# Linear attention and a 4-bit MLP on one core: the q and k projections as three one-pass products of exact 12-bit pieces

## The chip, the core and the metric

The kernel runs on one core of a Trainium2 chip. A core has a tensor engine (TensorE, PE in the profile, with its weight loads as PEld), a vector engine (DVE), a scalar engine (ACT), GpSimd (POOL) and a sync engine (SP), which here only issues DMA transfers. Each engine runs its own instructions in order and waits for the others through semaphores. SBUF is the working memory of 128 partitions; PSUM has eight banks and takes the results of TensorE. The metric is the device time of one execution in microseconds.

## The reference

Input x is (4, 512, 512): four batches of 512 tokens with 512 features. Two residual blocks follow each other, each on a layer norm of its input.

```python
# block 1: gated linear attention, 4 heads of 128, chunks of 128 tokens
q = (x @ Wq + bq); k = (x @ Wk + bk); v = (x @ Wv + bv)          # each 512 x 512
k = k / max(norm(k, axis=-1), 1e-12)                              # per head
alpha = sigmoid(x @ Walpha + balpha); beta = softplus(x @ Wbeta + bbeta)
# per chunk: attn = (q k^T) * beta * decay, causal;  y = attn v + (q state) * chunk_decay
#            state = state * total_decay + v^T (k * beta * decay_to_end)
# block 2: 4-bit GEGLU MLP, 512 -> 4096 -> 512
inter = gelu(x @ Wg.T) * (x @ Wu.T);  out = inter @ Wd.T
```

Wg, Wu and Wd come as 4-bit numbers with a scale per 32 elements, and are unpacked on the chip.

## The kernel before

The program has one list of steps, counted by `p`. The first 48 belong to the attention projections, 12 for each of the four batches `b`: steps `j` 0 to 3 compute v for one token tile of 128 (`product_v`), 4 to 7 compute q transposed for one head (`product_q`), 8 to 11 compute k for one token tile (`product_k`). Behind each step `behind(p)` emits the work of the attention chunk, which lags nine steps and takes three steps: with `p % 3 == 0` the transposed k (`chunk_lead`) and the decays (`chunk_decay`), with 1 the scores (`chunk_scores`), with 2 the sums (`chunk_sums`), the next chunk's factors (`chunk_values`) and the norm of the finished tile (`second_norm`). From batch 1 on the normed rows are turned by two DMA passes through DRAM and a DVE transpose (`cross`, `turn_blocks`); batch 0 and the second norm use TensorE transposes (`turn`). So the program's order on each engine is written by hand, and nothing else plans it.

The projections are float32 matmuls. The transposed normed rows of a batch stand in `hT[b]`, two tiles of 128 x 2 x 512; v (L425, L432) has them as stationary operand with 128 tokens, q (L450) has Wq as the stationary and all 512 tokens as the moving operand, k (L474) has the tokens stationary and Wk moving. ACT evicts q with its bias (L454), DVE evicts v (L440, L441) and k (L480).

The MLP follows. It works in rounds over the batches, with each gate/up tile (`gate_up`) as products that are already one-pass: the weights and the activations are split in three float32r pieces `hi`, `lo` and `mi`, and

```python
            for o, js in ((pa, (0, 1)), (pb, (2,))):
                for j in js:
                    for k in range(KC):
```

(L849 to L851) makes 8 + 4 matmuls in two PSUM banks; ACT takes `pb` with a factor (L858), DVE adds `pa` (L859). The first gate/up steps lie inside batch 3: after `j == 9` of that batch two steps of the MLP are put in, and from step 50 on only the MLP is left.

The MLP's weights are unpacked in the meantime. `fetch` loads one set of packed numbers and scales, `more` takes three `two_k` tiles for it if there are three (L243), and `unpack` emits one of the set's steps a call: `fields` (L162, two instructions), `masked` (L167), `scaled` (L171), `hi` on ACT (L177) with `lo` (L180), and `mi` (L183). Until step 49 `unpack` is called at L1080, in two steps of three from step 13 on.

SBUF tiles come from two lists of slots, `two_k` (24 of 128 x 2 x 512) and `one_k` (42 of 128 x 512, which borrow from `two_k` when they run out). A slot is handed out in the order in which it came free, and its new writer waits for the old readers. The eight PSUM banks go round in order too.

The functions that the change touches, and what calls them:

## Time and profile before

| | us |
|---|---|
| median of 3 runs | 1301.86 (1300.24 to 1302.41) |
| span of the profiled execution | 1299.2 |
| around the span, to the median | 2.7 |
| TensorE busy | 1287.6 |
| vector engine busy | 968.7 |
| q matmuls, L450 (64 in the program, 128 recorded) | 57.6 |
| k matmuls, L474 (64, 128 recorded) | 57.4 |
| last k matmul starts at | 234.2 |

For the profiled execution the profile gives the span from its first to its last instruction as its own time; what lies around it is taken as the distance to the median of the runs. The granted clock of TensorE is 1.00 throughout.

How to read the profile: the chain of work that ended last goes back from the last instruction to what released it, and its share by line says which line's time the program's time is made of. A table of stretches gives each engine's busy time between two points of the span. A timeline row has its start, its duration, the engine, the line, and how long the engine had been idle before it and for whom. Every float32 matmul is recorded as two instructions. Matmuls are pipelined, and their ends are modelled: the spacing of the chain's pieces says more than the single durations.

### The profile page before, as it was taken

Reading aid. Unit: us, or ns where it says so; the run is one execution under the profiler, and the core shown is the slowest. Engines: PE = TensorE matmul, PEld = TensorE weight load, DVE = VectorE, ACT = ScalarE, POOL = GpSimd, SP = SyncE. Lnnn points to the kernel's source line nnn. Section 1 sums busy time; section 2 is a strip of 40 time slices with the busy share of each in tenths; the row PEclk is TensorE's granted clock in tenths of the full one; section 3 lists DMA queues with packets and bytes.
Section 4 is the critical chain, followed back from the end, with each engine's and each line's share of the span. In section 5 each row is a group of like instructions: output and inputs, shape, how many; then the busy total and the mean of one; then the engine's idle time right before and its main releaser. Section 6 shows DMA issues by size and latency. Waiting matters only on the chain.

```text
span 1299.2 us, 17045 instructions
## 1 busy us (share of the span) xinstructions
PE 1287.6 (99%) x5736; PEld 1030.2 (79%) x5736; DVE 968.7 (75%) x1581; ACT 451.8 (35%) x878; POOL 113.1 (9%) x179
## 2 busy tenths in 40 slices
PE   9999999999999999999999999999999999999998
PEld 6667576778888888888888888888888888887886
DVE  4577865887777777777777777777777777777566
ACT  2433335743333333333333333333333333332332
POOL 1536362400000000000000000000000000000000
PEclk9999999999999999999999999999999999999999
DMA  6556667986565656565656565656565556555473
GB/s 206 148 168 196 191 196 223 314 279 205 179 195 178 195 178 195 178 195 178 195 178 195 178 194 179 195 178 195 178 194 179 192 181 192 180 179 199 167 253 126
DMA packets 195383, 250.24 MB, mean 193 GB/s; under 512 B 16672, under 2 KB 93792, under 8 KB 195296
## 3 DMA queue, kind: packets, MB, share of 16 engines
q1 hardware_dynamic: 195296, 249.16, 59.7%
q8 instruction: 45, 0.74, 0.2%
q14 instruction: 42, 0.34, 0.1%
HBM read 191.91 MB, written 57.18 MB: 192 GB/s over the span
## 4 chain that ended last, share of the span: by engine, by line
PE 95%; DMA 2%; DVE 1%; ACT 1%; SPq 0%; issue 0%; POOL 0%; DVEq 0%; ACTq 0%
PE pa L853 35%; PE p_d L897 26%; PE pb L853 17%; PE pq L450 4%; PE pk L474 4%; PE pvb L432 2%; PE pva L425 2%; PE yp L717 1%; PE sp L663 1%; PE yp L719 1%; PE dp L688 1%; PE tp_f L380 1%; DMA wvb<-in_Wv 0%; DMA x<-h 0%; DMA acc<-acc 0%
## 5 line engine op out<-in xcount | busy, mean ns | idle before, releaser
L853 PE MATMUL pa<-x,wgu 128*128 128x512 f32 x2048 | 507.1, 390 | 0.1
L853 PEld LDWEIGHTS pa<-x,wgu 128*128 128x128 f32 x2048 | 383.9, 188 | 79.5 <-DVE acc L909 0.4
L897 PE MATMUL p_d<-wd,i 128*128 128x512 f32 x1542 | 357.3, 389 | 2.3 <-DVE xr L726 0.6
L897 PEld LDWEIGHTS p_d<-wd,i 128*128 128x128 f32 x1542 | 288.3, 188 | 65.7 <-DVE i L877 2.1
L858 ACT ACTIVATE t<-pb 128x512 f32<-128x512 f32 x256 | 151.3, 591 | 356.5 <-PE pb L853 353.6
L853 PE MATMUL pb<-x,wgu 128*128 128x512 f32 x1024 | 273.8, 389 | 0.0
L859 DVE TENSOR_TENSOR t<-pa,t 128x512 f32<-128x512 f32 x256 | 176.6, 690 | 81.0 <-ACT t L858 75.7
L853 PEld LDWEIGHTS pb<-x,wgu 128*128 128x128 f32 x1024 | 192.3, 188 | 40.0
L905 DVE SCALAR_TENSOR_TENSOR acc<-p_d,acc 128x512 f32<-128x512 f32 (+1 forms) x137 | 93.4, 683 | 125.5 <-PE p_d L897 123.8
L873 ACT ACTIVATE i<-t 128x512 fp32r<-128x512 f32 x128 | 81.0, 633 | 194.3 <-DVE t L870 191.2
L865 ACT ACTIVATE t<-t 128x512 f32<-128x512 f32 x128 | 81.1, 634 | 136.2 <-DVE t L859 136.2
L877 DVE TENSOR_TENSOR i<-t,i 128x512 fp32r<-128x512 f32 x128 | 88.4, 691 | 25.9 <-ACT i L873 24.1
L909 DVE TENSOR_TENSOR acc<-acc,p_d 128x512 f32<-128x512 f32 x135 | 92.9, 688 | 14.4 <-PE p_d L897 0.5
L870 DVE SCALAR_TENSOR_TENSOR t<-t,t 128x512 f32<-128x512 f32 x128 | 88.6, 692 | 4.3
L928 POOL TENSOR_TENSOR acc<-acc,last 128x512 f32<-128x512 f32 x1 | 1.3, 1295 | 1015.0 <-ACT last L927 1015.0
L878 DVE SCALAR_TENSOR_TENSOR i<-i,t 128x512 fp32r<-128x512 f32 x128 | 89.0, 695 | 0.0
L450 PE MATMUL pq<-hT,wq 128*128 128x512 f32 x128 | 57.6, 595 | 0.0
L474 PE MATMUL pk<-wk,hT 128*128 128x512 f32 x128 | 57.4, 593 | 0.0
L450 PEld LDWEIGHTS pq<-hT,wq 128*128 128x128 f32 x128 | 23.6, 191 | 24.1 <-issue 23.9
L474 PEld LDWEIGHTS pk<-wk,hT 128*128 128x128 f32 x128 | 23.3, 191 | 23.9 <-issue 23.9
L183 DVE TENSOR_TENSOR wgu<-wgu,wgu 128x1024 fp32r<-128x1024 f32 x32 | 38.9, 1216 | 0.0
L180 DVE SCALAR_TENSOR_TENSOR wgu<-wgu,w_gu 128x1024 fp32r<-128x1024 f32 x32 | 38.9, 1215 | 0.0
(120 smaller groups left out, 902.0 us busy)
## 6 DMA issues: line engine op xcount, KB each, us to landing
x<-h SPq DMA_DIRECT2D x420, 256.0 KB
acc<-acc SPq DMA_DIRECT2D x256, 256.0 KB
h<-g SPq DMA_DIRECT2D x48, 256.0 KB
x<-in_x SPq DMA_DIRECT2D x16, 256.0 KB
pk_gu<-in_gate_p SPq DMA_DIRECT2D x32, 128.0 KB
sc_gu<-in_gate_s SPq DMA_DIRECT2D x64, 64.0 KB
pk_gu<-in_up_p SPq DMA_DIRECT2D x32, 128.0 KB
sc_gu<-in_up_s SPq DMA_DIRECT2D x64, 64.0 KB
```

The costliest lines, as they stand in the source:

```text
L450: nc.tensor.matmul(pq, f32(wq[k // 2])[:, k % 2, h * P : (h + 1) * P], f32(hT[b][k // 2])[:, k % 2, :], start=(k == 0), stop=(k == KC - 1),)
L474: nc.tensor.matmul(pk, f32(hT[b][k // 2])[:, k % 2, n * P : (n + 1) * P], f32(wk[k // 2])[:, k % 2, :], start=(k == 0), stop=(k == KC - 1),)
L853: nc.tensor.matmul(o, w3[j][:, k % 2, c * P : (c + 1) * P], x[j * KC + k], start=(j == js[0] and k == 0), stop=(j == js[-1] and k == KC - 1),)
L858: nc.scalar.activation(f32(t), pb, AF.Copy, scale=-1.0 / ONE_E)
L859: nc.vector.tensor_tensor(f32(t), pa, f32(t), ALU.add)
L865: nc.scalar.activation(f32(g), f32(g), AF.Gelu_apprx_tanh, scale=ONE_E)
L870: nc.vector.scalar_tensor_tensor(f32(u), f32(g), ONE_E, f32(u), ALU.mult, ALU.mult)
L877: nc.vector.tensor_tensor(il, f32(u), f32(ih), ALU.subtract)
L878: nc.vector.scalar_tensor_tensor(im, f32(ih), ONE_E, f32(u), ALU.mult, ALU.subtract)
L897: nc.tensor.matmul(banks[key_][:, part], inter[i][j][:, n * P : (n + 1) * P], wd[ms[i] // 2][j][:, ms[i] % 2, part], start=(i == 0 and j i ...
L905: nc.vector.scalar_tensor_tensor(a, banks[n, False, part.start][:, part], ONE_E, a, ALU.mult, ALU.add)
L909: nc.vector.tensor_tensor(a, a, banks[n, True, 0], ALU.subtract)
```

## The change

q and k are computed like the MLP's gate and up products. The operands are split into pieces of 12 bits: `hi` is the operand rounded to 12 bits by ACT's output type, `lo` is the rest, and `mi` is `hi` less the (scaled) rest, so that hi·hi + lo·lo (in `pa`) and mi·mi (in `pb`) together give the product. `three` makes 12 one-pass matmuls for each product where 4 float32 matmuls stood.

- The transposed normed rows of a token tile go to a raw `one_k` tile `rows_of[b, n]`; v takes it as it is. `pieces` makes `hi` (ACT), `lo` and `mi` (both DVE) from it, in halves of 128 x 256, for four token tiles in the steps 0, 1, 2 and 2 of a batch. `hT[b]` becomes six `two_k` tiles instead of two. `read` frees the raw tile when v and the pieces have read it.
- `split` makes the pieces of Wq in steps 1 and 2 of batch 0 (128 x 1024 at a time: ACT, DVE, POOL), and those of Wk in steps 4 to 7 (128 x 512 at a time). Wq's pieces are six `two_k` tiles, Wk's are twelve `one_k` tiles; the raw ones come free.
- q's eviction becomes an ACT instruction on `pb` and a DVE instruction on `pa`. k's becomes an ACT instruction on `pb`, a POOL addition of the bias and a DVE addition of `pa`; k is left with a factor that the norm takes away.
- `two_k` has 25 tiles. `more` starts a set of MLP weights only if `kept` further `two_k` tiles are free, and from step 40 on `unpack` is called twice in two steps of three and once in the third.

```diff
@@ -117,7 +117,7 @@
                 else:
                     self.free.append(tag)
 
-    two_k = Homes("a", 24, [P, 2, T])
+    two_k = Homes("a", 25, [P, 2, T])
     one_k = Homes("b", 42, [P, T], two_k)
 
     def psum(name):
@@ -240,7 +240,7 @@
 
     def more():
 
-        if not loaded or len(two_k.free) < 3:
+        if not loaded or len(two_k.free) < 3 + kept(place[0]):
             return
         nxt, start = loaded.pop(0)
         fields, masked, scaled, hi, lo, mi = start()
@@ -273,6 +273,50 @@
     VA = D + 2 * H - D // 2
     VB = D - VA
     acc, hT, q_sb, k_sb, v_sb = {}, {}, {}, {}, {}
+    rows_of, half_read = {}, set()
+
+    def kept(p):
+
+        if p > 3 * NCH * (B - 1) + NCH:
+            return 2 if p < 3 * NCH * B else 0
+        return H // 2 + (3 * KC // 2 if p % (3 * NCH) == 0 and p < 3 * NCH * B else 0)
+
+    def split(hi, lo, mi, w):
+
+        nc.scalar.activation(hi, w, AF.Copy, scale=HI * E12)
+        nc.vector.scalar_tensor_tensor(lo, f32(hi), -4096.0, w, ALU.mult, ALU.add)
+        nc.gpsimd.tensor_tensor(mi, f32(hi), f32(lo), ALU.subtract)
+
+    def pieces(b, n):
+
+        if n == 0:
+            hT[b] = [[two_k.get(f"h{j}_{b}_{c}") for c in range(KC // 2)] for j in range(3)]
+        r = rows_of[b, n]
+        for c in range(KC // 2):
+            hi, lo, mi = (hT[b][j][c][:, :, n * P : (n + 1) * P] for j in range(3))
+            w = f32(r)[:, 2 * c * P : 2 * (c + 1) * P].rearrange("p (two t) -> p two t", two=2)
+            nc.scalar.activation(hi, w, AF.Copy, scale=HI * 4096.0)
+            nc.vector.scalar_tensor_tensor(lo, w, 4096.0, f32(hi), ALU.mult, ALU.subtract)
+            nc.vector.scalar_tensor_tensor(mi, f32(hi), E12, f32(lo), ALU.mult, ALU.subtract)
+        read(b, n)
+
+    def read(b, n):
+
+        if (b, n) in half_read:
+            one_k.put(rows_of.pop((b, n)))
+        half_read.add((b, n))
+
+    def three(key, w, x, soon=False):
+
+        pa, pb = psum(f"pa_{key}"), psum(f"pb_{key}")
+        for o, js in ((pa, (0, 1)), (pb, (2,))) if soon else ((pb, (2,)), (pa, (0, 1))):
+            for j in js:
+                for k in range(KC):
+                    nc.tensor.matmul(
+                        o, w(j, k), x(j, k),
+                        start=(j == js[0] and k == 0), stop=(j == js[-1] and k == KC - 1),
+                    )
+        return pa, pb
 
     def round_now():
         while rounding:
@@ -382,20 +426,17 @@
             use(tp)
 
     def first_norm(b, n, src, within=None):
-        if n == 0:
-            hT[b] = [two_k.get(f"hT{b}_{c}") for c in range(KC // 2)]
-
         soon = b == n == 0
 
         def use(tp):
-            for c in range(KC // 2):
-                to = f32(hT[b][c])[:, :, n * P : (n + 1) * P]
-                new = tp[:, 2 * c * P : 2 * (c + 1) * P].rearrange("p (two t) -> p two t", two=2)
-                for part in ((0, 1), (1, 2)) if soon else ((0, 2),):
-                    nc.scalar.copy(to[:, slice(*part), :], new[:, slice(*part), :])
+            r = rows_of[b, n] = one_k.get(f"r_{b}_{n}")
+            w = P if soon else D
+            for i in range(0, D, w):
+                nc.scalar.copy(f32(r)[:, i : i + w], tp[:, i : i + w])
 
         def way(t):
-            turn_blocks(t, *(f32(hT[b][c])[:, :, n * P : (n + 1) * P] for c in range(KC // 2)))
+            r = rows_of[b, n] = one_k.get(f"r_{b}_{n}")
+            turn_blocks(t, heads(f32(r)))
 
         norm(src, f"a{b}_{n}", use, 2 if soon else 1, within, way if b > 0 else None)
 
@@ -419,20 +460,21 @@
 
     def product_v(b, n, between=None):
 
-        toks = slice(n * P, (n + 1) * P)
+        r = f32(rows_of[b, n])
         pa, pb = psum(f"pva_{b}_{n}"), psum(f"pvb_{b}_{n}")
         for k in range(KC):
             nc.tensor.matmul(
-                pa[:, :VA], f32(hT[b][k // 2])[:, k % 2, toks], f32(wva[k // 2])[:, k % 2, :VA],
+                pa[:, :VA], r[:, k * P : (k + 1) * P], f32(wva[k // 2])[:, k % 2, :VA],
                 start=(k == 0), stop=(k == KC - 1),
             )
         if between:
             between()
         for k in range(KC):
             nc.tensor.matmul(
-                pb[:, : VB + 2 * H], f32(hT[b][k // 2])[:, k % 2, toks], wvb_[:, k, :],
+                pb[:, : VB + 2 * H], r[:, k * P : (k + 1) * P], wvb_[:, k, :],
                 start=(k == 0), stop=(k == KC - 1),
             )
+        read(b, n)
         v = one_k.get(f"v_{b}_{n}")
         v_sb[b, n] = v
         if n == 0:
@@ -445,15 +487,15 @@
 
         if h == 0:
             q_sb[b] = [two_k.get(f"q{b}_{c}") for c in range(H // 2)]
-        pq = psum(f"pq_{b}_{h}")
-        for k in range(KC):
-            nc.tensor.matmul(
-                pq, f32(wq[k // 2])[:, k % 2, h * P : (h + 1) * P], f32(hT[b][k // 2])[:, k % 2, :],
-                start=(k == 0), stop=(k == KC - 1),
-            )
-        nc.scalar.activation(
-            f32(q_sb[b][h // 2])[:, h % 2, :], pq, AF.Identity, bias=bq_sb[:, h : h + 1]
+        pa, pb = three(
+            f"q_{b}_{h}",
+            lambda j, k: wq[j][k // 2][:, k % 2, h * P : (h + 1) * P],
+            lambda j, k: hT[b][j][k // 2][:, k % 2, :],
+            b == h == 0,
         )
+        q = f32(q_sb[b][h // 2])[:, h % 2, :]
+        nc.scalar.activation(q, pb, AF.Identity, bias=bq_sb[:, h : h + 1], scale=-1.0)
+        nc.vector.scalar_tensor_tensor(q, pa, ONE_E, q, ALU.mult, ALU.add)
 
     def far(b, n):
 
@@ -469,15 +511,18 @@
 
     def product_k(b, n):
 
-        pk = psum(f"pk_{b}_{n}")
-        for k in range(KC):
-            nc.tensor.matmul(
-                pk, f32(hT[b][k // 2])[:, k % 2, n * P : (n + 1) * P], f32(wk[k // 2])[:, k % 2, :],
-                start=(k == 0), stop=(k == KC - 1),
-            )
+        pa, pb = three(
+            f"k_{b}_{n}",
+            lambda j, k: hT[b][j][k // 2][:, k % 2, n * P : (n + 1) * P],
+            lambda j, k: wk[j][k],
+        )
+        t = one_k.get(f"kt_{b}_{n}")
+        nc.scalar.activation(f32(t), pb, AF.Copy, scale=-1.0 / ONE_E)
+        nc.gpsimd.tensor_tensor(f32(t), f32(t), f32(bk_sb), ALU.add)
         kt = one_k.get(f"k_{b}_{n}")
         k_sb[b, n] = kt
-        nc.vector.tensor_tensor(heads_of(kt, far(b, n)), in_blocks(pk), in_blocks(f32(bk_sb)), ALU.add)
+        nc.vector.tensor_tensor(heads_of(kt, far(b, n)), in_blocks(pa), in_blocks(f32(t)), ALU.add)
+        one_k.put(t)
         if far(b, n):
 
             def use(t):
@@ -498,7 +543,7 @@
                 AF.Square, accum_out=sn[:, h : h + 1],
             )
         one_k.put(sq)
-        nc.gpsimd.tensor_scalar(sn, sn, 1e-24, None, ALU.max)
+        nc.gpsimd.tensor_scalar(sn, sn, 1e-24 / ONE_E**2, None, ALU.max)
         nc.gpsimd.tensor_tensor(sn, sn, minus_half, ALU.pow)
         brn = small.tile([P, H], F32, tag="brn", name=f"brn{b}_{n}")
         nc.gpsimd.tensor_tensor(brn, sn, beta[b][:, n * H : (n + 1) * H], ALU.mult)
@@ -1005,6 +1050,7 @@
         wvb = two_k.get("wvb")
         wvb_ = f32(wvb).rearrange("p two (k n) -> p (two k) n", n=VB + 2 * H)
         wq, wk = ([two_k.get(f"w{nm}{c}") for c in range(KC // 2)] for nm in "qk")
+        raw_q, raw_k = wq, wk
         x0 = [load(tile_of(n), f"x0_{n}") for n in range(2)]
 
         busy = psum("busy")
@@ -1043,6 +1089,8 @@
         turn("a", 1)
         blocks = mlp()
         p = 0
+        wq = [[two_k.get(f"wq{j}_{c}") for c in range(KC // 2)] for j in range(3)]
+        wk = [[one_k.get(f"wk{j}_{k}") for k in range(KC)] for j in range(3)]
         for b in range(B):
             for j in range(3 * NCH):
                 later = None
@@ -1061,23 +1109,47 @@
                     product_q(b, j - NCH)
                 else:
                     later = product_k(b, j - 2 * NCH)
+                if b == 0:
+                    if 0 < j < 3:
+                        split(*(wq[i][j - 1] for i in range(3)), f32(raw_q[j - 1]))
+                        two_k.put(raw_q[j - 1])
+                    if j < 3:
+                        pieces(0, j)
+                    if j == 2:
+                        pieces(0, 3)
+                    if j == NCH:
+                        nc.gpsimd.tensor_scalar(f32(bk_sb), f32(bk_sb), 1.0 / ONE_E, None, ALU.mult)
+                    if NCH <= j < 2 * NCH:
+                        k = j - NCH
+                        split(*(wk[i][k] for i in range(3)), f32(raw_k[k // 2])[:, k % 2, :])
+                        if k % 2:
+                            two_k.put(raw_k[k // 2])
+                elif j < 3:
+                    pieces(b, j)
+                    if j == 2:
+                        pieces(b, 3)
                 if b == B - 1:
                     if j == NCH - 1:
                         two_k.put(*wva, wvb)
                         one_k.put(bv_sb)
                     elif j == 2 * NCH - 1:
-                        two_k.put(*wq)
+                        for ws in wq:
+                            two_k.put(*ws)
                     elif j == 3 * NCH - 1:
-                        two_k.put(*wk)
+                        for ws in wk:
+                            one_k.put(*ws)
                         one_k.put(bk_sb)
                 if j == 3 * NCH - 1:
-                    two_k.put(*hT[b])
+                    for hs in hT[b]:
+                        two_k.put(*hs)
                 behind(p)
                 if later:
                     later()
                 if p in (5, 7):
                     fetch()
-                if p > 3 * NCH and p % 3:
+                if p > 3 * NCH * (B - 1) + NCH - 1:
+                    unpack(2 if p % 3 else 1, MT)
+                elif p > 3 * NCH and p % 3:
                     unpack(1, MT)
                 p += 1
                 if b == B - 1 and j in (2 * NCH - 4, 2 * NCH - 3):
```

## The prediction

> **What bounds the kernel now.** I read the page's busy shares first, then the chain, then the stretches of the attention stage, then the tensor engine's timeline beside the vector engine's.
>
> ```profile
> PE 1287.6 (99%) x5736; PEld 1030.2 (79%) x5736; DVE 968.7 (75%) x1581; ACT 451.8 (35%) x878; POOL 113.1 (9%) x179
> ...
> PE 95%; DMA 2%; DVE 1%; ACT 1%; SPq 0%; issue 0%; POOL 0%; DVEq 0%; ACTq 0%
> PE pa L853 35%; PE p_d L897 26%; PE pb L853 17%; PE pq L450 4%; PE pk L474 4%; PE pvb L432 2%; PE pva L425 2%; PE yp L717 1%; PE sp L663 1%; PE yp L719 1%; PE dp L688 1%; PE tp_f L380 1%; DMA wvb<-in_Wv 0%; DMA x<-h 0%; DMA acc<-acc 0%
> ```
>
> TensorE (PE) is busy 99% of 1299.2 us and carries 95% of the chain; the products that change (L450, L474) carry 8% of it. All of them lie before 235 us. The chain prices one product of each kind, the float32 ones and the three one-pass products of the MLP (L853), whose shapes the new ones take:
>
> ```profile
> 45.70 3.44 PE pk L474 x8
> ...
> 50.02 3.44 PE pk L474 x8
> ...
> 276.98 1.81 PE pa L853 x8
> 278.79 0.91 PE pb L853 x4
> ...
> 280.13 1.85 PE pa L853 x8
> 281.98 0.91 PE pb L853 x4
> ```
>
> 3.44 us for four float32 matmuls (recorded as eight), 2.72 to 2.76 us for twelve one-pass matmuls. What pays for it is the vector engine (DVE). The stretches (columns: start and end, length, then busy time with the number of instructions of PE, PEld, DVE, ACT and POOL, the granted clock, DMA) show the first batch from its first q product, the four three-step cycles of the second, and the place where attention ends and the MLP starts:
>
> ```profile
> 23.70:38.40 14.70, 14.70 (x39) 6.56 (x39) 6.81 (x30) 5.78 (x12) 0.55 (x1) 1.00 0.33 92
> 38.40:55.28 16.88, 16.88 (x61) 9.19 (x61) 5.87 (x13) 7.05 (x36) 6.96 (x14) 1.00 0.63 170
> 55.28:70.25 14.97, 14.97 (x89) 13.48 (x88) 10.18 (x27) 4.48 (x16) 10.78 (x17) 1.00 0.47 143
> 70.25:84.60 14.35, 14.35 (x69) 10.02 (x68) 12.16 (x31) 4.58 (x11) 5.92 (x7) 1.00 0.62 184
> 84.60:99.03 14.43, 14.43 (x60) 8.14 (x59) 10.94 (x29) 7.04 (x20) 3.38 (x5) 1.00 0.57 172
> 99.03:112.88 13.85, 13.85 (x57) 8.03 (x56) 10.12 (x20) 6.00 (x32) 10.92 (x19) 1.00 0.81 221
> ...
> 200.50:273.00 72.50, 69.11 (x338) 49.52 (x337) 53.34 (x97) 44.24 (x110) 24.12 (x37) 1.00 0.85 274
> ```
>
> TensorE never stops in the first six; DVE is busy 68% to 85% of the second batch, and the last stretch already holds 3.4 us of stalled TensorE.
>
> **The sum.** It is made against the profiled execution: span 1299.2 us, and 2.7 us more to the median of the runs, 1301.86, which I leave as they are.
>
> *Products.* 16 q and 16 k products go from 3.44 to 2.74 us: 32 x 0.70 = 22.4 us gained, all on the path. The v products keep their instructions. [...]
>
> *Prices on DVE.* By distance of starts in its timeline: 128x256 with two inputs 0.34 us (L440 to L441), 128x512 0.61 (L407 to L408), 128x1024 1.1 (L180 to the next). New there: `pieces`, 4 of 128x256 per token tile, 16 x 0.34 = 5.4 us a batch; the second half of q's eviction, 4 x 0.61 = 2.4 a batch; once, `lo` of Wq, 2 x 1.1, and of Wk, 4 x 0.61. One 128x512 transpose in place of two halves returns 0.07 a tile. ACT's part (0.6 for a 128x512 copy, some 6 us a batch) lies beside its 35%.
>
> *The added wait.* k's addition on DVE (L480) now waits for ACT's copy (0.6, L858) and POOL's bias (1.04 to 1.30, L642 and L928) of the part that TensorE ends 1.85 us before the other. They fit, if POOL is free. Behind the addition stand on DVE the chunk's sum (L726) and the norm's statistics; ACT's squares (L496) and the transposes of k (L593) wait for it, the latter a whole product (2.7 us) later. That cover makes it nothing; without it POOL's power for the squares (L502, 1.04 to 1.41 in front of the bias) would cost up to 1 us a product, 0 to 16 in all, which I leave to rival 2. Each product takes two of the eight PSUM banks; DVE may lag three products before a bank is missing, and it lags less.
>
> *Batch 0.* Its eight products save 5.6 us. Against that, DVE's queue in program order:
> - `pieces(0,0)` (1.4) pushes the third token tile's norm, so its transposes come 0.4 us late.
> - After the sums of v's third tile (20.6) come `lo` of Wq and the pieces of two tiles; with what is pushed down from before, DVE is through at about 26, where it began the norms of batch 1 at 20.63. q's first product starts at 24.1 and needs those pieces only in its second third, so it loses nearly nothing.
> - The norms (3.6), v's last sums (0.9) and the gates' first two (0.3) then end at 30.6, where they ended at 25.2. ACT stands in order behind them: two q evictions and two `hi` of Wk (2.4), the table (1.28), the logarithm: 35.0. TensorE is at the gate sums (L560) at 32.6: 2.4 us lost.
> - q's evictions and `lo` of Wk for the last k wait behind the rest of the gates and the third norm: 41.6, plus 1.04 on POOL for `mi` (a 128x512 row there, L642). TensorE is there at 39.4 (35.1 + 0.9 for the gate sums + 2.7 for the last q + 0.7 for three quarters of k's `mi` part, which comes first): 3.3 us lost.
> - The row sums of the gates are sent some 2.4 us later, behind the next tile's way and five weight loads on SP's queue; the k waits cover all but 0.3.
>
> Sum 6.4. Whether POOL's `mi` holds DVE up no row of this stage shows. The nearest: L878 took 1.53 us at 229.96 instead of 0.69 while POOL ran L642 (229.72 to 230.93). POOL takes two `mi` of 128x1024, by L642 some 2.1 us each, before q's first product: between 0 and 4.2 us. I take 1, since v's sums, about half of DVE's work beside them, read PSUM, and the rows of that kind (L440) show no such delay. Batch 0 loses 7.4 (2 to 11) of its 5.6: it ends about 2 us later.
>
> [...]
>
> *Batch 1.* The cycles' DVE work becomes 10.2 + 5.4 = 15.6, 12.2 + 1.2 = 13.4, 10.9 + 1.2 = 12.1 and 10.1; TensorE's becomes 15.0, 12.9, 12.2, 11.8 (0, 2, 3 and 3 products shorter). In the first two DVE is over by 1.1, and it keeps a wait of 0.44 a cycle for POOL's power (L341). The path leaves some 2 us between the scores and their use. I take 2.0 lost (0 to 5, the latter if POOL's 4.5 us of 128x512 work a cycle block the pieces).
>
> *Batches 2 and 3 up to q.* The slots of `two_k`: 25 less 3 for Wv, 6 for Wq's pieces, 6 for h's and 2 to 4 for q leave 6 to 8, where 24 less 3, 4, 2 to 4 and 2 to 4 left 9 to 13. With the reserve of `kept` only two sets of three are unpacked before step 43; the sets gate/up 1 and 2, unpacked in steps 25 to 41 so far (by L162 to L183 0.75 + 0.65 + 3 x 1.2 = 5.0 us each), come in steps 43 to 49. That takes 10 us off DVE here and covers the pieces (2 x 7.6): 1.0 lost (0 to 3).
>
> *Steps 43 to 53 (200 to 273 us).* They get these 10.1 us and 1.2 of q: DVE 53.3 + 11.3 = 64.6, in TensorE's 69.1 less six products' 4.2 = 64.9. DVE is full where it had waits of its own (19 us idle in 72.5). Beside it the 42 `one_k` tiles run short: with 12 held for Wk and the raw tiles, I count 3 free at step 45 and none at 48 (five `two_k` stand in), where 15 and 11 were; so writers wait for transfers that still read, as POOL did for 4.92 us before L642 at 229.72. The moved weights' loads pass SP's queue here too, 5 issues of about 0.55 a set. 5 us lost (1 to 10), half of the added work, since the deadlines (gate/up 1 at step 52, 2 at 58) are kept. From step 54 on the order of unpacking is as before, and nothing is counted.
>
> Sum: -22.4 + 7.4 + 2.0 + 1.0 + 5.0 = -7.0 us; 1301.9 becomes **1295**. The lower ends of the costs (3) give 1282.5, the upper ones (29) 1308.5.
>
> **The rivals.**
> 1. *Nearly all of it is hidden.* For: TensorE has no stall before 164 us, and DVE is only 43% busy from 23.7 to 38.4. Against: the gates and Wk's last piece are late by counted queues. Only 4 us are lost: 1283.
> 2. *POOL and DVE block each other: slower.* New POOL work is 2 x 2.1 + 4 x 1.04 + 16 x 1.04 for k's bias = 25 us, all two-input, and 22 us of pieces meet the old POOL rows. For: 229.96, and L349 with 1.44 for 0.74 at 74.58 under L612 and L621. Against: most POOL work stands in stretches where DVE reads PSUM. Over 8 us of blocking that reaches TensorE it is slower than before; at 15 us in place of my 1 it is 1309.
> 3. *The MLP starts late.* Steps 43 to 53 lose 13 in place of 5, from tiles that are not free: 1303. For: such waits stand there with 15 tiles free. Against: TensorE stalled only 3.4 us in all.
>
> That one-pass products are no shorter I rule out by L853, which has the same shape and type.
>
> **How the numbers follow.** Forecast 0.45 (its own range 1288 to 1301), rival 1 0.15, rival 2 0.26, rival 3 0.14. The bound of no change is 0.2%, 2.6 us, about what a measurement of this kernel can tell. Faster: 0.40 + 0.15 + 0.02 = 0.57; same 0.05 + 0.01 + 0.06 = 0.12; slower 0.25 + 0.06 = 0.31. The range 1283 to 1309 leaves out half of rival 1 and under half of rival 2.
>
> **What would show it.** q and k products of 2.7 us in the chain; the first q near 24; waits of TensorE at L560 near 33 and at the first k near 39; DVE over 95% busy in 55 to 108 with few us of stall; unpacking of gate/up 1 and 2 behind q's last product; stalls over 3.4 us between 200 and 270; from there on the same spacing as before. Wrong it is if DVE's 128x256 pieces last over 0.5 us on average (rival 2), if k's addition waits for POOL by over a microsecond a time, or if TensorE meets no wait before 60 us (rival 1).

## The result, and the profile after

The changed kernel takes **1361.37 us** (median of 4, 1360.9 to 1362.72); the kernel before took 1301.05 in the same session. The ratio is 1.0466, interval 1.0451 to 1.0481: 60 us slower, where 7 us faster was forecast and 1309 was the upper end.

The page after, its busy shares, clock and chain:

```profile
span 1361.0 us, 17526 instructions
...
PE 1292.9 (95%) x5864; PEld 1069.8 (79%) x5864; DVE 1022.1 (75%) x1655; ACT 474.5 (35%) x929; POOL 145.9 (11%) x202
...
PEclk9899999988999999999999999999999999999999
...
PE 80%; DVE 8%; DMA 4%; POOL 3%; issue 2%; ACT 1%; SPq 1%; DVEq 0%; ACTq 0%; POOLq 0%
```

TensorE stood idle for 11.6 us before; now it is 1361.0 - 1292.9 = 68 us. Its busy time hasn't fallen either, since parts of it ran at a lower granted clock: 1.00 throughout before, mean 0.979 after. The chain is no longer TensorE's alone: DVE, DMA and POOL hold 15% of it.

The stretches (start and end, length, busy time and instructions of PE, PEld, DVE, ACT and POOL, clock, DMA share, GB/s) of the first batch from its first q products, of the span of which I had said that DVE would be over 95% busy, and of the end of attention; then the last 600 us:

```profile
24.00:43.50 19.50, 13.38 (x53) 9.89 (x51) 17.56 (x42) 6.84 (x13) 7.77 (x7) 0.91 0.19 54
43.50:67.70 24.20, 17.08 (x77) 13.63 (x76) 9.75 (x21) 9.14 (x37) 13.67 (x20) 0.85 0.47 131
55.00:108.00 53.00, 44.82 (x234) 37.98 (x232) 38.19 (x89) 20.78 (x70) 28.83 (x40) 0.94 0.54 160
...
248.00:347.00 99.00, 77.28 (x379) 64.02 (x379) 70.07 (x117) 48.46 (x113) 27.23 (x39) 0.88 0.67 211
```

```profile
762.00:1358.00 596.00, 594.20 (x2617) 489.91 (x2616) 449.94 (x661) 193.84 (x313) 1.29 (x1) 1.00 0.56 186
```

Of these stretches only the first has DVE nearly full (90%). In 43.5 to 67.7 it works 9.75 of 24.2 us, while TensorE stands for 7.1: both wait for something else. In the last 596 us the kernel runs as before (2617 matmuls where the kernel before has 2618), so the 60 us are lost before 350. The list of waits names what DVE, ACT, TensorE and POOL stood for (who waited for whom: us in all, times, the longest):

```profile
DVE k L524 <- POOL kt L521: 43.6, 12, 10.6
...
ACT sq L541 <- DVE k L524: 30.2, 11, 3.7
PE yp L762 <- DVE dm L719: 28.8, 9, 9.3
...
POOL kw L687 <- DMA h<-g: 14.0, 2, 7.0
...
ACT L653 <- DMA acc<-xr: 7.9, 1, 7.9
```

k's addition waits for POOL's bias 12 times, 3.6 us a time. The chunk's masked scores `dm` stand behind it on DVE, and TensorE's `yp` waits for `dm`. ACT and POOL wait for stores that still read the tile which they are to overwrite (`h<-g`, `acc<-xr`).

### The profile page after: what moved, and what is told of

The parts are those of the page before. It is cut to its first block, busy times and chain, and to the rows that moved or that the text cites. A ratio compares the mean times of both kernels' runs of the same rounds, so it can differ in the third digit from the quotient of the medians.

```text
span 1361.0 us, 17526 instructions
## 1 busy us (share of the span) xinstructions
PE 1292.9 (95%) x5864; PEld 1069.8 (79%) x5864; DVE 1022.1 (75%) x1655; ACT 474.5 (35%) x929; POOL 145.9 (11%) x202
## 4 chain that ended last, share of the span: by engine, by line
PE 80%; DVE 8%; DMA 4%; POOL 3%; issue 2%; ACT 1%; SPq 1%; DVEq 0%; ACTq 0%; POOLq 0%
PE pa L898 34%; PE p_d L942 25%; PE pb L898 17%; PE pa_q L315 1%; DVE h L300 1%; DMA h<-g 1%; DMA acc<-xr 1%; DVE h L299 1%; PE pb_q L315 1%; DMA x<-h 1%; POOL kt L521 1%; POOL ss L547 1%; PE pa_k L315 1%; PE sp L708 1%; PE yp L762 0%
## 5 line engine op out<-in xcount | busy, mean ns | idle before, releaser
L762 PE MATMUL yp<-vb,dm 128*128 128x128 f32 x128 | 26.8, 314 | 28.8 <-DVE dm L719 28.8
L524 DVE TENSOR_TENSOR k<-pa_k,kt 128x512 f32<-128x512 f32 x16 | 11.0, 688 | 47.8 <-POOL kt L521 43.6
L762 PEld LDWEIGHTS yp<-vb,dm 128*128 128x128 f32 x128 | 21.4, 219 | 31.4 <-issue 16.7
L171 DVE SCALAR_TENSOR_TENSOR w_gu<-i_gu,sc_gu 128x1024 f32<-128x1024 f16 x32 | 38.9, 1215 | 0.0
```

What stands on the lines that cost most here:

```text
L762: nc.tensor.matmul(yp[:, hs], f32(dm)[:, hs], f32(vb)[:, hs], start=True, stop=(n == 0))
```

## The experiments

Each is timed against the kernel before on the same chip. The first eight undo one part or show one alone, the next seven take the parts away one after the other or undo several at once, and the last three turn to what held the time before the change.

### k's link: factors later; eviction by DVE alone

The squares and POOL's factors of each k tile one step later, against the changed kernel:

```
+                while pending:
+                    pending.pop(0)()
                 behind(p)
                 if later:
-                    later()
+                    if b == B - 1 and j in (2 * NCH + 1, 3 * NCH - 1):
+                        later()
+                    else:
+                        pending.append(later)
```

> The changed kernel (1361.4 us) with the squares and the POOL factors of each k tile sent one step later, behind the eviction of the next product. Everything is computed. Theory 'loop': with k's addition on DVE now behind ACT's copy and POOL's bias, and these two in order behind the factors of the tile before, each k tile goes round a chain of 5.1 to 6.3 us where TensorE brings one every 2.7; the k stages of the four batches lost 10, 8.7, 5 and part of 18 us, and the clock that falls after the stalls is in these. Sending the factors late opens the ring: 25 to 34 us gained, about 1330, and the additions of k 2.7 to 4 us apart. Rival 'tiles' (writers wait for transfers that still read) and rival 'DVE full': the order of the factors matters little, under 8 us gained, 1353 or more.

Measured 1357.3, ratio 1.0435 (1.042 to 1.0451): 4 us gained. The loop, as I had drawn it, falls: with the order of the factors changed DVE still waits for the bias,

```profile
DVE k L524 <- POOL kt L521: 30.2, 7, 9.4
```

since POOL has other work in front of it, `kw`, `vb` and the mask. So the next run takes ACT and POOL out of the link:

```
-        nc.scalar.activation(f32(t), pb, AF.Copy, scale=-1.0 / ONE_E)
-        nc.gpsimd.tensor_tensor(f32(t), f32(t), f32(bk_sb), ALU.add)
+        nc.vector.scalar_tensor_tensor(f32(t), pb, -1.0 / ONE_E, f32(bk_sb), ALU.mult, ALU.add)
```

> The changed kernel (1361.4 us), k's eviction by DVE alone: t = pb times -1/E plus the bias, then pa + t; ACT's copy and POOL's bias leave the chain. Everything is computed. DVE gets 16 x 0.69 = 11 us more work and waits for TensorE only. Sending the factors late gave 4 us, so the order of the factors is not the loss. Theory 'waits' (DVE stands at the head of its queue for POOL's bias, 43.6 us in the trace of after, with the scores' product dm behind it, for which TensorE waits 28.8): 15 to 30 us gained with the clock that falls after each stall, 1331 to 1346. Theory 'DVE full': more work there, same or up to 11 us slower.

Measured 1345.2, ratio 1.0328 (1.0305 to 1.0351): **16 us gained, though DVE is busy 8 us longer (1030.3 against 1022.1).** It is the wait, not DVE's load; nor is it chiefly that POOL's bias blocks DVE, since the new work is 16 x 0.69 = 11 us and only some 3 us of other work got shorter. TensorE's wait for `dm` falls from 28.8 to

```profile
PE yp L761 <- DVE dm L718: 15.5, 7, 4.2
```

### q alone, k alone

In the first k is float32 from the raw rows, with Wk uncut (and 27 and 38 tiles in the two lists instead of 25 and 42); in the second q and v are float32 from a float32 hT, with Wq uncut:

```
-        pa, pb = three(
-            f"k_{b}_{n}",
...
+        r = f32(rows_of[b, n])
+        pk = psum(f"pk_{b}_{n}")
...
-        pa, pb = three(
-            f"q_{b}_{h}",
...
+        pq = psum(f"pq_{b}_{h}")
```

> q alone as one-pass products; k stays float32 from the raw rows, with its bias added by DVE as before; no pieces of Wk. Everything is computed. The products then give 11.2 us instead of 22.4. Theory 'loop': the losses of the k stages go (24 us in the first three batches, and most of the 18 at the start of the MLP), those of the q and v stages (8, 10.8, 12.8, 3.2) stay: 1301 - 11 + 35 = about 1325, with no wait of DVE for POOL's bias. Rival 'DVE full': pieces and q's second eviction are still there, so most of the loss stays: 1340 or more.

> k alone as one-pass products; q and v stay float32 from a float32 hT, from which the pieces are cut; no pieces of Wq. Everything is computed. Theory 'loop': k's chain is all there, q's second eviction and Wq's pieces are not; 11.2 us of products gained, the four k stages lose some 45 and the pieces about 10: about 1350. Rival 'DVE full' (q's second halves and Wq's pieces push it over): 1320 or less.

Measured 1331.0, ratio 1.0236 (1.0216 to 1.0255), for q alone and 1356.0, 1.0423 (1.0405 to 1.044), for k alone: k's part is the dear one, by 25 us, as the waits said; the tiles that each of the two holds differ too, and the pair doesn't separate that. But q alone is 30 us slower than before too, without any wait for POOL's bias, so there are more causes.

### The moved unpacking alone, the added work alone

Both start from the kernel before. The first moves the unpacking of gate/up 1 and 2:

```
-        if not loaded or len(two_k.free) < 3:
+        if not loaded or len(two_k.free) < 3 or len(wgu) + len(wd) > 1 and place[0] < 44:
...
-                if p > 3 * NCH and p % 3:
+                if p > 3 * NCH * (B - 1) + NCH - 1:
+                    unpack(2 if p % 3 else 1, MT)
+                elif p > 3 * NCH and p % 3:
```

> The kernel before (float32 products) with only the unpacking moved: the sets gate/up 1 and 2 are unpacked from step 44 on, as in the changed kernel, instead of in steps 25 to 41. Everything is computed. My prediction's term for that is 5 us (1 to 10) with the short tiles: about 1306 by it. Theory 'tiles': the tiles are not short here, and DVE has room, so the move alone costs under 2 us: 1303 or less. Rival 'DVE full' in steps 43 to 53: half of the moved 10 us and more, 1306 to 1311.

Measured 1312.5, ratio 1.0091 (1.0066 to 1.0116): 12 us, not my 5. DVE is no fuller (970.9 us against 968.7). The loads that go with the moved sets stand on SP's queue in front of the loads of `acc`, and the transposes of k wait behind DVE for these, 4.8 of the 12 us:

```profile
PE tpk L593 <- DVE acc L905: 4.8, 1, 4.8
DVE acc L905 <- DMA acc<-acc: 4.3, 1, 4.3
```

The second makes the pieces of h in the kernel before and throws them away:

```
+            nc.scalar.activation(hi_, w, AF.Copy, scale=HI * 4096.0)
+            nc.vector.scalar_tensor_tensor(lo_, w, 4096.0, f32(hi_), ALU.mult, ALU.subtract)
+            nc.vector.scalar_tensor_tensor(mi_, f32(hi_), E12, f32(lo_), ALU.mult, ALU.subtract)
```

> The kernel before (1300.5 us), with the work of the pieces alone: after each token tile ACT's two 128x256 copies and DVE's four 128x256 two-input operations, into three tiles that are given back at once and read by nobody. Everything is computed; q and k stay float32. It adds 4 x 5.4 to 7.6 us to DVE and no wait for TensorE. Theory 'DVE full': the added work pushes the scores' dm behind it; 10 to 25 us slower, 1310 to 1325. Theory 'waits': the work itself fits beside TensorE, under 4 us slower, 1304 or less.

Measured 1313.4, ratio 1.0093 (1.0062 to 1.0123): some 12 us slower (8 to 16), though DVE has room in the sum. The pieces stand in its queue ahead of `dm`.

### POOL and DVE at the same time

```
-        nc.gpsimd.tensor_tensor(mi, f32(hi), f32(lo), ALU.subtract)
+        nc.vector.tensor_tensor(mi, f32(hi), f32(lo), ALU.subtract)
```

> The changed kernel with the third piece of Wq and Wk (mi) made by DVE in place of POOL. Everything is computed. Theory 'lock' (a 128x256 piece lasts 2.47 us in place of 0.42 while POOL works on mi, and TensorE waits 4.49 and 5.0 us in batch 0): the stalls at 28.9, 47.4 and 49.9 us shrink from 9.5 to some 5, since DVE must now do 2 x 1.1 + 4 x 0.6 itself, and the half clock after the first one goes: 4 to 8 us gained, 1353 to 1357, with pieces of 0.42 us there. Rival 'DVE full in batch 0': no gain, 1360 to 1366.

In the changed kernel's timeline of DVE (start, length) one piece is held until POOL's `mi` is over, which runs from 19.47 for 2.48 us:

```profile
19.31 0.42 DVE L299 SCALAR_TENSOR_TENSOR h<-r,h 128x256 fp32r<-128x256 f32 x1
19.76 2.47 DVE L300 SCALAR_TENSOR_TENSOR h<-h,h 128x256 fp32r<-128x256 f32 x1
```

With `mi` on DVE:

```profile
20.05 0.42 DVE L299 SCALAR_TENSOR_TENSOR h<-r,h 128x256 fp32r<-128x256 f32 x1
20.50 0.42 DVE L300 SCALAR_TENSOR_TENSOR h<-h,h 128x256 fp32r<-128x256 f32 x1
```

The blocking is real (a second time at 25.26, 2.44 us), and dear per instruction. It is mutual: POOL's `vb` (L695) takes 1.22 us beside a piece, twice, and 1.04 to 1.07 us in its other ten runs. Taking `mi` off POOL gives little: 1358.5, ratio 1.0438 (1.0412 to 1.0464), 3 us gained and hardly clear of the intervals, since DVE then makes `mi` itself. In the rows both pieces end 0.28 us behind POOL's `mi`, less than the 0.42 us that such a piece takes alone.

The run takes away only the blocking under `mi`. With `mi` on DVE the second and third pieces still last 0.56 and 0.55 us on average (behind the bar: busy us, mean ns),

```profile
L299 DVE SCALAR_TENSOR_TENSOR h<-r,h 128x256 fp32r<-128x256 f32 x32 | 18.0, 564 | 0.2 <-ACT h L298 0.2
L300 DVE SCALAR_TENSOR_TENSOR h<-h,h 128x256 fp32r<-128x256 f32 x32 | 17.7, 554 | 1.1
```

so by 0.42 us a piece some 9 us of DVE's time are still lost in them. In the changed kernel's trace, the two under `mi` left aside, 14 of the 64 second and third pieces take 0.83 to 1.26 us, 8.8 us over 0.42 in all, and each runs beside POOL's work on the chunk (L657 to L695) for at least three quarters of its length; the 36 that meet no POOL instruction take 0.40 to 0.43. How much of that reaches TensorE no run shows.

### The granted clock

After seven of the eight stalls over 2.5 us in the first 350 us the granted clock is 0.50 for 3.1 to 6.1 us behind them. TensorE, in the stall that ends at 137.1 and behind it, in the changed kernel:

```profile
132.00:135.00 3.00, 0.20 (x2) 0.01 (x1) 0.53 (x1) 0.31 (x1) 2.36 (x4) 1.00 0.00 0
135.00:137.00 2.00, 0.00 (x0) 0.00 (x0) 2.00 (x5) 1.75 (x9) 0.30 (x2) 0.59 0.43 126
137.00:142.00 5.00, 4.90 (x15) 4.23 (x16) 3.21 (x6) 1.42 (x10) 2.76 (x4) 0.50 0.63 181
```

The next run fills four stalls with matmuls that nobody reads:

```
         yp = psum(f"yp_{b}_{n}")
+        for _ in range({(1, 0): 16, (2, 0): 13, (3, 1): 33}.get((b, n), 0)):
+            nc.tensor.matmul(yp[:, :P], ident, ident, start=True, stop=True)
...
         tp = psum(f"tpk_{b}_{n}")
+        for _ in range(20 if (b, n) == (3, 3) else 0):
+            nc.tensor.matmul(tp[:, :P], ident, ident, start=True, stop=True)
```

> The changed kernel with work added to TensorE alone: 16, 13 and 33 float32 matmuls 128x128 that nobody reads, ahead of the products yp which stalled 4.90, 4.05 and 9.29 us, and 20 ahead of the transposes that stalled 5.76, each row some 0.9 of its stall long (0.245 us a matmul by the scores' rows). Everything is computed. Theory 'clock' (a stall of some 3 us halves the granted clock for the next 4 to 6 us, so it costs about half as much again): the clock stays 1.0 there, and the kernel is 6 to 11 us faster with 20 us of work more: 1350 to 1355. Rival (the clock falls for another reason, or falls all the same): within 2 us of 1361, or slower by what the added matmuls overshoot, up to 5 us.

```profile
132.00:137.00 5.00, 5.00 (x38) 4.66 (x37) 0.62 (x2) 1.79 (x8) 4.18 (x7) 1.00 0.03 12
137.00:142.00 5.00, 4.43 (x31) 3.98 (x31) 3.28 (x7) 1.76 (x9) 3.05 (x5) 1.00 0.49 138
```

The clock stays at 1.00 here, and behind the second filling too (1.00 in 205 to 208 and 208 to 213, where the changed kernel has 0.84 and 0.75), so it does follow the stall. But the time is 1368.8, ratio 1.051 (1.049 to 1.053): 7 us slower. Of these, 6 are the fourth filling's: its stall is one for a PSUM bank, so the filling stood in it too and ran behind it, from 325.89 to 331.88. The other three gave nothing back, and the next stall is longer (`yp` at 159.1 waits 4.13 where it waited 2.95 at 156.9). By that, TensorE at half clock was in the first two places spending time that it would have waited, and the low clock is a mark of the loss and not a cause of its own.

At the last stall, the one whose filling failed, it is a cause. From 324.03 to the MLP's steady part TensorE never waits again in the changed kernel, and begins at half clock:

```profile
324.03:329.93 5.90, 5.90 (x16) 4.76 (x17) 5.02 (x8) 3.67 (x7) 1.50 (x2) 0.50 0.67 253
```

Half of 5.90 us is some 3 us of the 60, an estimate from this row and from the eight first matmuls of a `yp`, which take 2.04 us at 0.50 (207.04) and 1.13 at 1.00 (208.35 with the stall filled).

### Taking the parts away one by one

First the cutting of Wq and Wk, with all tiles held; then its tiles too; then k's eviction by DVE as above. Where a piece is left out, the first piece stands in for it, so these kernels don't compute the reference's q and k:

```
-            lambda j, k: wk[j][k],
+            lambda j, k: wk[0][k],
...
-                        split(*(wk[i][k] for i in range(3)), f32(raw_k[k // 2])[:, k % 2, :])
+                        nc.scalar.activation(wk[0][k], f32(raw_k[k // 2])[:, k % 2, :], AF.Copy, scale=HI * E12)
...
-        wk = [[one_k.get(f"wk{j}_{k}") for k in range(KC)] for j in range(3)]
+        wk = [[one_k.get(f"wk{j}_{k}") for k in range(KC)] for j in range(1)]
```

(and the same for Wq).

> The changed kernel without the cutting of Wq and Wk: DVE's and POOL's two operations a piece are left out, ACT's first piece stands in for all three, so q and k are not the reference's; all tiles are held as before, and every product and eviction runs. It prices what the cutting of the weights costs in batch 0. Theory 'batch 0 late by the cutting': the stalls at 28.9, 47.4 and 49.9 us (9.5 us) go, with the half clock behind them (some 6 us of it lost in 28 to 54): 10 to 16 us gained, 1345 to 1351. Rival (the wait moves on to the next chunk's dm, as filling TensorE's stalls showed, where 5 us less of lost clock gave nothing): under 5 us gained, 1356 or more.

> As the kernel without the cutting, and the tiles of the second and third pieces of Wq and Wk aren't held either: 4 more of two_k and 8 more of one_k are free through all four batches (and one more set of gate/up weights fits before step 43). What it gains over the kernel without the cutting is what short tiles cost: DVE, ACT and POOL waited 42.5 us for stores of h and of xr that still read a tile in the trace of after, 11.6 in that of before. Theory 'tiles': those waits fall to some 12 us and 12 to 25 us more are gained: 1325 to 1338. Rival 'waits for POOL and a full DVE are all': under 5 us more, 1343 to 1350.

> As the kernel with neither cutting nor its tiles, with k's eviction by DVE alone. All three causes taken away: the cutting, the short tiles, DVE's wait for POOL (16 us by itself). If they add up: about 16 us less than the kernel without cutting and tiles, 1309 to 1322, and what is left over the 1280 that the products alone would give is the pieces of h (11 us measured on the kernel before), the moved unpacking and q's second half. If they overlap (one wait hides behind the other): 1320 to 1340.

Measured 1351.2, ratio 1.0394 (1.0378 to 1.0411); 1332.6, 1.0252 (1.0236 to 1.0267); 1314.5, 1.011 (1.0095 to 1.0125). **They add up.** The cutting costs 10 us, short tiles 19, k's link 18 (16 by itself). With the tiles free the waits of ACT and POOL for stores of h and xr go from 42.5 us (11 waits, in 20 to 350; 11.6 us in the kernel before) to one of 1.1:

```profile
POOL rs_a L385 <- DMA acc<-xr: 1.1, 1, 1.1
```

Free tiles also let one more set of weights be unpacked early, so the 19 us hold a part of the move.

Of versions that compute everything, the three edits to the changed kernel together:

> The changed kernel with the three edits that compute everything put together: k's eviction by DVE, mi by DVE, factors sent late (16, 3 and 4 us by themselves). If they add up: 1338. If they overlap, 1342 to 1345, since the factors waited for the same k addition. Neither theory has it under 1310.

Measured 1339.9, ratio 1.0309 (1.0292 to 1.0326): 21.5 us gained, nearly the 23 that the three gave one by one. It doesn't reach the kernel before, nor does q alone (1331).

The next three take away, in turn, DVE's pieces of h; their tiles and the moved unpacking; and the second half of q's eviction:

```
-            nc.vector.scalar_tensor_tensor(lo, w, 4096.0, f32(hi), ALU.mult, ALU.subtract)
-            nc.vector.scalar_tensor_tensor(mi, f32(hi), E12, f32(lo), ALU.mult, ALU.subtract)
...
-        if not loaded or len(two_k.free) < 3 + kept(place[0]):
+        if not loaded or len(two_k.free) < 3:
...
-                if p > 3 * NCH * (B - 1) + NCH - 1:
-                    unpack(2 if p % 3 else 1, MT)
-                elif p > 3 * NCH and p % 3:
+                if p > 3 * NCH and p % 3:
...
-        nc.scalar.activation(q, pb, AF.Identity, bias=bq_sb[:, h : h + 1], scale=-1.0)
-        nc.vector.scalar_tensor_tensor(q, pa, ONE_E, q, ALU.mult, ALU.add)
+        nc.scalar.activation(q, pa, AF.Identity, bias=bq_sb[:, h : h + 1], scale=ONE_E)
```

> The kernel without cutting and its tiles and with k's eviction by DVE (1314.5 us), and without DVE's two pieces of h: ACT's first piece stands in for all three, so q and k are not the reference's; the tiles of the other two pieces are held. 4 x 16 x 0.34 = 22 us of DVE's work leave. By what the same work cost on the kernel before (11 us): 1303 to 1305. If DVE has room there once its waits are gone: 1310 or more. If the pieces stand in front of everything in the first cycles of each batch: 1298 or less.

> As the kernel without the pieces, their tiles not held, and the unpacking in the order of the kernel before (gate/up 1 and 2 unpacked before step 43). By what the move cost on the kernel before (11 to 12 us): some 11 us less, 1291 to 1294. If that cost came from the stall at k's transposes alone (4.8 us), which the freed tiles have already taken away: under 5 us less.

> As the kernel before it in this list, and q's eviction in one ACT instruction as in the kernel before (the first part alone, so q lacks its last piece's product, which TensorE still makes). What is left of the change is then its products and k's two DVE additions. If the account is complete, the products' 22.4 us are there: 1279 to 1283 with an idle TensorE of some 7 us. If q's second half costs something, it is the difference to the run before; by DVE's prices (16 x 0.61 = 10 us of work) 3 to 8 us. If 1290 or more is left, a cause is still missing.

Measured 1302.9, ratio 1.0017 (1.0007 to 1.0027); 1303.4, 1.0021 (1.0009 to 1.0034); 1303.8, 1.0027 (1.0016 to 1.0037). The pieces cost 11.6 us, about what they cost on the kernel before, their blocking by POOL included. The other two give nothing more. And here the account closes on the wrong number: the four parts sum to 10.2 + 18.6 + 18.1 + 11.6 = 58.5 us, nearly the whole 60, and the kernel stops at the time of the one before. The 22 us of shorter products are nowhere, though they are made. In the last of these runs:

```profile
PE 1273.3 (98%) x5864; PEld 1054.6 (81%) x5864; DVE 975.7 (75%) x1585; ACT 465.6 (36%) x913; POOL 110.7 (8%) x180
```

TensorE's busy time is 14 us less than before (the ends of matmuls are modelled; the spacing in the chain gives the 22), and it idles 1302.8 - 1273.3 = 29.5 us.

### Were the products on the path at all?

Two runs of the kernel before, with nothing added, moved or taken away but a part of the contraction:

```
-        for k in range(KC):
+        for k in range(3):
...
-                start=(k == 0), stop=(k == KC - 1),
+                start=(k == 0), stop=(k == 2),
```

(in q and in k; with 2 and 1 in the second run).

> The kernel before with the last quarter of the contraction left out of the q and k products: three float32 matmuls in place of four, 32 x 0.86 = 27.5 us less for TensorE, and no other instruction added, moved or taken away. If the products are on the path, as the prediction's first term has it: 1273 to 1278. If the chunk's own chain (scores, dm, yp, with what stands ahead on DVE and SP's queue) is as long as TensorE's work, as the last three runs suggest: 1290 to 1301, with TensorE idle by 15 to 28 us more.

> The same with half of the contraction left out, 32 x 1.72 = 55 us less for TensorE. If the products are on the path: some 1248 to 1255. If another chain is as long: no more gained than with three quarters, within 5 us of it.

Measured 1302.2, ratio 1.0016 (1.0006 to 1.0026), and 1299.1, 0.9992 (0.9982 to 1.0002). **Taking 27 or 55 us of products away from a TensorE that is 99% busy gains nothing that can be measured (+2 and -1 us).** The waits of TensorE with three quarters, and with half:

```profile
PE yp L717 <- DVE dm L674: 13.8, 8, 3.9
PE sp L663 <- DVE kT L326: 2.7, 2, 1.7
```

```profile
PE yp L717 <- DVE dm L674: 24.4, 9, 6.5
PE sp L663 <- DVE kT L326: 4.7, 4, 1.9
```

The granted clock doesn't explain that. It is 0.996 and 0.989 on the mean of the profiled executions, some 5 and 14 us of their spans, so it takes a part of what was saved; but in the run before these it is 0.999, and that one gains nothing either.

Nor are the chunks earlier with half than with three quarters: the `yp` of the second starts at 64.86 against 63.63, that of the twelfth at 205.04 against 204.55, with some 25 us less of products for TensorE by then (29 of the 32, 0.86 us each). Something else spaces them.

Back from one of the waits, the `yp` of the first chunk (three quarters; ACT, then DVE, then TensorE):

```profile
46.68 1.28 ACT L608 ACTIVATE dm<-sums,ncla 128x128 f32<-128x128 f32 x4 [6.39 <-DMA sums<-rows]
```

```profile
48.70 0.69 DVE L674 TENSOR_TENSOR dm<-sp,dm 128x512 f32<-128x512 f32 x1 [5.72 <-POOL dm L612]
```

```profile
49.45 1.16 PE L717 MATMUL yp<-vb,dm 128*128 128x128 f32 x8 [2.84 <-DVE dm L674]
```

A second chain runs beside TensorE's, and by these runs it is about as long: the gates' row sums come back through DRAM, ACT makes the decays, POOL masks them, DVE multiplies the scores. In the kernel before ACT waited for the row sums too (first line; three quarters in the second), but TensorE came just as late, so nothing showed:

```profile
ACT dm L608 <- DMA sums<-rows: 18.4, 4, 5.3
```

```profile
ACT dm L608 <- DMA sums<-rows: 29.9, 6, 8.3
```

That is in 4 and 6 of the 16 chunks; what sets the others wasn't followed. Still, with three quarters the chunks ran ahead: the `yp` of the twelfth chunk starts at 204.55 where it started at 212.98. By the sixteenth only 1.8 of these 8.4 us are left (270.49 against 272.30). In that stretch the kernel before has a DMA share of 0.92, with three quarters it is 0.89 (the granted clock is 0.93 there, some 3 us of the stretch):

```profile
226.40:273.00 46.60, 43.21 (x224) 32.87 (x223) 38.29 (x65) 30.65 (x70) 15.94 (x22) 1.00 0.92 299
```

```profile
226.40:273.00 46.60, 42.14 (x210) 32.26 (x209) 34.71 (x62) 27.12 (x63) 14.02 (x22) 0.93 0.89 288
```

The last run, also with three quarters, takes transfers out of it. In the MLP's first three rounds the second and third piece of its operand x aren't loaded, and the first stands in for them:

```
-                x3[i].append(load(h2d[i % B][j][k], f"x_{i}_{j}_{k}"))
+                if i < 3 and j > 0:
+                    x3[i].append(one_k.get(f"x_{i}_{j}_{k}"))
+                else:
+                    x3[i].append(load(h2d[i % B][j][k], f"x_{i}_{j}_{k}"))
```

> The kernel before with three quarters of the contraction of q and k (1302 us, TensorE idle 23 us), and without 20 of the 36 loads of the MLP's operand x in its first three rounds: the first of the three pieces stands in for the other two there, whose tiles are held; so the output is not the reference's. 5 MB less in the stretch before and at the start of the MLP. If transfers hold the MLP's start: the 8 us that the chunks are ahead at step 36 arrive, and perhaps more: 1288 to 1295. If the chunk's chain through ACT, DVE and POOL holds it: within 3 us of the run with three quarters, 1299 to 1304.

```profile
226.40:273.00 46.60, 44.11 (x244) 36.50 (x243) 41.11 (x71) 30.31 (x68) 14.54 (x21) 1.00 0.72 223
```

Measured 1292.8, ratio 0.9933 (0.991 to 0.9956): 9 us less than with all loads, and the only run clearly below the kernel before (by leaving work out). The twelfth `yp` starts at 207.89 and the sixteenth at 263.20. So with the chunks ahead, these transfers hold the MLP's start; the clock, at 1.00 here, can have a part in it. Whether it is their bytes or their issues on SP's queue the run doesn't tell: 24 loads are left out (396 of `x<-h` in place of 420; the expectation says 20). Nor is there a run that leaves them out with all products made. What would follow in the first three batches if the row sums came sooner wasn't tried.

## Why the prediction was wrong

| step of the sum | predicted, us | measured, us | run |
|---|---|---|---|
| products 3.44 to 2.74 | -22.4 | 0 (+2 for three quarters, -1 for half) | three quarters, half |
| k's addition waits for ACT and POOL | 0 | +16 to +18 | k by DVE, twice |
| tiles short, unpacking moved | +6.0 (1.0 and 5.0) | +19 (move alone on the kernel before 12) | tiles freed; moved |
| Wq, Wk cut, gates late in batch 0 | +7.4 | +10 | no cutting |
| pieces of h in batch 1 (later ones covered) | +2.0 | +12 in all batches | added work; no pieces |

**The first term failed, and by the most.** The duration was right, 0.92 + 1.82 = 2.74 us in the chain of the kernel with free tiles and k's eviction by DVE:

```profile
236.24 0.92 PE pb_k L315 x4
237.16 1.82 PE pa_k L315 x8
```

What was wrong was "all on the path". I read a chain of 95% TensorE and a busy share of 99% as if every microsecond of TensorE were worth one. The chain shows one path that ended last, and another of about the same length lay beside it. The views held a hint: ACT waited for row sums, and the stretch in front of the MLP, which I quoted, had a DMA share of 0.85. I used its DVE column and left that one unread. Of the rivals none said that the gain itself was not there.

**"They fit, if POOL is free" failed next.** POOL is 9% busy on the page, and it isn't free at k's addition: in front of the bias on its queue stand `kw`, `vb`, the mask and the factors of the tile before, which wait for ACT, which waits for DVE. I had set this wait's price aside as "0 to 16 in all, left to rival 2", and it came to 16 to 18. The sign that I gave for it (over a microsecond a time) showed 3.6.

**Rival 2** was on the right side, and its cause is at most a part. POOL and DVE do block each other (2.47 us for 0.42 on DVE, 1.22 for 1.04 on POOL; the 32 second and third pieces last 0.56 and 0.68 on average, over my mark of 0.5), but `mi` on DVE gives back 3 us only. The pieces' blocking under POOL's old work, which the rival named too (8.8 us of DVE's time in the changed kernel), lies in the 12 us of the pieces and wasn't taken apart from their work. **Rival 3** named the tiles, and its 13 us are near what the freed tiles give back, but by luck: those 19 are of all batches, and it spoke of steps 43 to 53.

**Batch 0** was near in size and not in place. The first q product came at 23.1 (said: near 24), but its second third waited 4.49 us, where I had it lose nearly nothing; the first k waited 3.3 and 1.7 near 47 to 50, not at 39. **DVE over 95% busy in 55 to 108** was wrong: 38.2 of 53 us, 72%. I counted DVE's work against TensorE's time, and most of the costs came from order and waits, with DVE idle. **Unpacking behind q's last product** cost more than its DVE work, by its loads on SP's queue, which I had counted as five issues a set (they are six) and not followed to the `acc` loads behind them. From the last stretch on the spacing was the same, as said.

## What to carry to other kernels

Before crediting a shorter instruction, ask what else ends at the same time: shorten it alone, by leaving a part of it out, and see whether the time moves. In this balanced kernel the answer was lopsided: an addition off TensorE cost much of its price (22 us of pieces on DVE, by the prices of the prediction, cost 12), and a saving on one engine gave nothing while another chain was as long (27 and 55 us of products less: +2 and -1 us). A helper on a nearly idle engine was not free either (POOL was 9% busy, and k's addition behind it cost 16 us); what counted was the queue in front of it at that moment, and who was in order behind the one that waited.

## What was unexpected of the hardware

The granted clock after stalls. It was 1.00 before, and after single stalls of TensorE of 2.1 to 9.3 us, or shorter ones close together, it was mostly 0.50 for the next 3 to 6 us. In the trace's record of the clock six of the eleven low stretches last 3.41 us, four 6.83 and one 10.24. No length of stall decides it alone: 2.11 us idle before 66.47 brought 0.50 from 67.1 to 70.5, while 2.95 us before 156.85 left it at 1.00. What decides it no run shows. That a lower clock must cost time isn't so: with the clock held at 1.00 behind two stalls the kernel was no faster (1368.8 us against 1361.4, of which some 6 us are the fourth filling's). It cost some 3 us, by the estimate above, where no wait followed.

```profile
64.30:66.40 2.10, 0.06 (x1) 0.00 (x0) 1.36 (x3) 0.64 (x5) 0.70 (x1) 1.00 0.01 4
...
67.00:70.00 3.00, 3.00 (x12) 2.48 (x11) 0.00 (x0) 0.52 (x2) 2.71 (x5) 0.52 0.46 129
```
